# Attention scores with keys on partitions and no row maximum, with the old code behind a branch, in a kernel of four attention layers

## The chip, the cores and the metric

One core of a Trainium2 chip. The metric is the device time of one execution in microseconds (us). Each kernel ran several times; medians are given. The numbers of a profile come from one profiled execution. The granted clock is the share of TensorE's full clock in the profile's clock records; "half clock" is 0.50 there. One run of the kernel before took 6055 us at a clock of 0.63 and is left out as slow.

## The reference

The input x is 4 x 512 channels x 1024 positions, fp32. Four layers update it one after another:

```python
# layer 0: attention, 8 heads of 64
qkv = x^T @ Wp.T + bp;  attn = softmax(q k^T * 64**-0.5);  x = x + (attn v) @ Wo.T + bo
# layer 1: linear attention, softplus features of width 64, gated by max + mean of each channel
x = x + gamma * (Qf @ (Kf^T V)) / (Qf @ (sum(Kf) + 1e-6))
# layer 2: layer norm over channels, attention with 1 head of 512, projection, residual
# layer 3: group norm (32 groups), attention with 4 heads of 128, projection, residual
```

`softmax` is jax.nn.softmax, so it is right for scores of any size.

## The kernel before

x stays on chip with channels on partitions. Per batch, q and k are made with channels on partitions and v with tokens on partitions. The attention holds scores with **queries** on partitions, so that the row maximum and the row sum run along the free axis, and must then transpose the normalised weights for the product with v:

```python
        def scores(i):                      # one tile of 128 queries x 1024 keys
            ...
            ps = ps_sc.tile([P, S], F32, tag="sc", name="sc")
            for half in range(NTB):
                for n, c in enumerate(chunks):
                    nc.tensor.matmul(ps[:, bass.ts(half, TB)],                       # L186
                        lhsT=q[p0:p1, c, bass.ts(qb * QT + t, P)], rhs=k[p0:p1, c, bass.ts(half, TB)], ...)
            nc.vector.tensor_reduce(nmax, ps, AX.X, ALU.max, negate=True)            # L193
            nc.scalar.activation(pr, ps, AF.Exp, bias=nmax, accum_out=rs)            # L196
            nc.vector.reciprocal(ri, rs)
            nc.vector.tensor_scalar(pr, pr, ri, None, ALU.mult)                      # L199

        def transposes(i):
            for half in range(2):
                ps = ps_tr.tile([P, NT // 2, P], F32, tag="tr", name="tr")
                for j in range(NT // 2):
                    nc.tensor.transpose(ps[:, j, :], pr[:, ...], ident)              # L212
                ... copied to pt by ScalarE (L215) or VectorE (L217)

        def values(qb, h):                  # after four query tiles
            for c in chunks:
                ps = acc_tile()
                for j in range(NT):
                    nc.tensor.matmul(ps[p0:p1, :],                                   # L227
                        lhsT=v[:, j, c * P + p0 : c * P + p1], rhs=pt[...], ...)
                nc.scalar.activation(ots[qb][p0:p1, c, :], ps[p0:p1, :], AF.Identity, bias=...)

        def project_out(qb): ...            # 4 x 4 matmuls (L243) and x += (L248)
```

The projections are L141 (q, k) and L156 (v). The tiles that matmuls write are two accumulators of 512 columns (`acc`), two score tiles of 1024 and two transpose tiles of 512. `head_rows` gives layer 0's 64-wide heads partitions 0 to 63 or 64 to 127 of a chunk, so there the stationary operand of the scores is 64x128 and that of the values 128x64.

The framework orders the instructions of each engine at compile time, nearly as written, but not always.

Of the kernel before, what the change touches and what calls it, by code (L numbers as in the profile page):

```python
# [11 lines left out]

F32 = mybir.dt.float32
AF = mybir.ActivationFunctionType
ALU = mybir.AluOpType
AX = mybir.AxisListType

P = 128
B = 4
C = 512  # L20
S = 1024
NC = C // P  # channel chunks
NT = S // P  # token tiles
TB = 512  # token block
NTB = S // TB
QT = TB // P
M = 64  # feature width of the linear attention
GROUP = 16  # channels in a group of the group norm

# Vectors over channels, each stored as columns of 128.  # L30
COLS = [
    ("bqkv0", 12),
    ("bo0", 4),
# [8 lines left out]
COL = {}  # L42
for _name, _n in COLS:
    COL[_name] = sum(n for _, n in COLS[: len(COL)])
NCOLS = sum(n for _, n in COLS)


@with_exitstack
def conv_seq(ctx: ExitStack, tc: tile.TileContext, d: dict, out: bass.AP):
    """x stays on chip, channels on partitions, and the four layers update it in place."""  # L50
    nc = tc.nc

    const = ctx.enter_context(tc.tile_pool(name="const", bufs=1))
# [2 lines left out]
    work = ctx.enter_context(tc.tile_pool(name="work", bufs=1))  # L56
    small = ctx.enter_context(tc.tile_pool(name="small", bufs=4))
    PSUM = bass.MemoryType.PSUM
    ps_acc = ctx.enter_context(tc.tile_pool(name="ps_acc", bufs=2, space=PSUM))
    ps_sc = ctx.enter_context(tc.tile_pool(name="ps_sc", bufs=2, space=PSUM))  # L60
    ps_tr = ctx.enter_context(tc.tile_pool(name="ps_tr", bufs=2, space=PSUM))

    def acc_tile():
        return ps_acc.tile([P, TB], F32, tag="acc", name="acc")

# [1 line left out]
    def load_wqkv(src, split=False):  # L67
        t = wpool.tile([P, NC, 3 * C], F32, tag="wqkv", name="wqkv")
        v = src.rearrange("(c p) o -> p c o", p=P)
        if split:  # L70
            return t, v
        nc.sync.dma_start(t, v)
        return t

    def load_wo(src):
        t = wpool.tile([P, NC, C], F32, tag="wo", name="wo")
        nc.sync.dma_start(t, src.rearrange("(c p) o -> p c o", p=P))
        return t
# [22 lines left out]
    gamma = const.tile([P, 1], F32, name="gamma")  # L101
    nc.sync.dma_start(gamma, d["gamma"].partition_broadcast(P))

# [1 line left out]
    ident = const.tile([P, P], F32, name="ident")  # L105
    make_identity(nc, ident)
    ones = const.tile([P, P], F32, name="ones")
    nc.vector.memset(ones, 1.0)
    eps = const.tile([P, 1], F32, name="eps")
    nc.vector.memset(eps, 1e-5)  # L110
    # gmat[p, m] = 1/16 where p and m lie in the same group of 16 channels
    gmat = const.tile([P, P // GROUP, GROUP], F32, name="gmat")
    nc.vector.memset(gmat, 1.0 / GROUP)
    nc.gpsimd.affine_select(
# [8 lines left out]
    def col(name, c, p0=0, p1=P):  # L123
        return cols[p0:p1, COL[name] + c : COL[name] + c + 1]

# [1 line left out]
    def project_qkv(wqkv, bias, scale, src):  # L127
        """q (scaled) and k with channels on partitions, v with tokens on partitions.

        src(tb) gives the input as a [P, NC, TB] block. v's bias is added to the attention's  # L130
        output instead, as each row of the softmax sums to one.
        """
        q = work.tile([P, NC, S], F32, tag="q", name="q")
        k = work.tile([P, NC, S], F32, tag="k", name="k")
        v = work.tile([P, NT, C], F32, tag="v", name="v")
        for tb in range(NTB):
            xb = src(tb)
            for o in range(2 * NC):
                ps = acc_tile()
                for c in range(NC):  # L140
                    nc.tensor.matmul(  # L141
                        ps, lhsT=wqkv[:, c, bass.ts(o, P)], rhs=xb[:, c, :],
                        start=(c == 0), stop=(c == NC - 1),
                    )
                if o < NC:
                    nc.vector.tensor_scalar(  # L146
                        q[:, o, bass.ts(tb, TB)], ps, col(bias, o), scale, ALU.add, ALU.mult
                    )
                else:
                    nc.scalar.activation(  # L150
                        k[:, o - NC, bass.ts(tb, TB)], ps, AF.Identity, bias=col(bias, o)
                    )
            for t in range(QT):
                ps = acc_tile()
                for c in range(NC):
                    nc.tensor.matmul(  # L156
                        ps, lhsT=xb[:, c, bass.ts(t, P)], rhs=wqkv[:, c, 2 * C : 3 * C],
                        start=(c == 0), stop=(c == NC - 1),
                    )
                if t % 2:  # L160
                    nc.scalar.copy(v[:, tb * QT + t, :], ps)
                else:
                    nc.vector.tensor_copy(v[:, tb * QT + t, :], ps)  # L163
        return q, k, v

    def attention(b, q, k, v, heads, bias, wo, bo, hooks, last):
        hd = C // heads
        nk = max(1, hd // P)
        x = xs[b]
# [1 line left out]
        probs, pts, ots = {}, {}, {}  # L171

        def head_rows(h):
            """The chunks of channels that hold head h, and its partitions in them."""
            if hd >= P:
                return [h * nk + i for i in range(nk)], 0, P
            per = P // hd
            return [h // per], (h % per) * hd, (h % per + 1) * hd
# [70 lines left out]
                if last:  # L249
                    nc.sync.dma_start(xout[b, :, o, bass.ts(qb, TB)], xv)  # L250

        # The scores run two steps ahead of the transposes that need their softmax, and the
        # products with v one step behind the transposes.
        n, due = len(items), {}
        i = 0
        while i < n + 2 or due:
# [15 lines left out]
    def attention_layer(wqkv, wo, bias, bo, heads, norm=None, after_qkv=None, last=False):  # L272
        scale = float(C // heads) ** -0.5
        steps = NTB * heads * QT
        ready = {}

        def normed(b, tb):
            ready[b, tb] = norm(b, tb)

        if norm is not None:  # L280
            for tb in range(NTB):
                normed(0, tb)
        for b in range(B):
            if norm is None:
                src = lambda tb: xs[b][:, :, bass.ts(tb, TB)]
            else:
                src = lambda tb: ready.pop((b, tb))
            q, k, v = project_qkv(wqkv, bias, scale, src)
            hooks = {}
            if norm is not None and b + 1 < B:  # L290
                for tb in range(NTB):
                    hooks[steps // 2 + tb * steps // 4] = lambda tb=tb: normed(b + 1, tb)
            if b == B - 1 and after_qkv is not None:
                after_qkv()
            attention(b, q, k, v, heads, bias, wo, bo, hooks, last)

# [1 line left out]
    attention_layer(wqkv, wo, "bqkv0", "bo0", heads=8)  # L298

# [1 line left out]
    wqkv = load_wqkv(d["wqkv2"])  # L301
    wo = load_wo(d["wo2"])
    bv1 = work.tile([P, C], F32, tag="pr", bufs=2, name="bv1")
    nc.sync.dma_start(bv1, d["bv1"].partition_broadcast(P))

    def softplus(z, e, u, l):
        """z <- max(z, 0) + log1p(exp(-|z|)), with log1p(e) = ln(u) + (e - (u - 1)), u = 1 + e."""
        nc.vector.scalar_tensor_tensor(e, z, -1.0, z, ALU.mult, ALU.min)
        nc.scalar.activation(e, e, AF.Exp)
        nc.vector.tensor_scalar(u, e, 1.0, None, ALU.add)  # L310
        nc.scalar.activation(l, u, AF.Ln)
        nc.vector.scalar_tensor_tensor(u, u, 1.0, e, ALU.subtract, ALU.subtract)
        nc.vector.tensor_tensor(l, l, u, ALU.subtract)
        nc.vector.scalar_tensor_tensor(z, z, 0.0, l, ALU.max, ALU.add)

    def linear_attention(b):
        x = xs[b]
        # queries [M, S], channels on partitions
        qbuf = work.tile([P, NC, S], F32, tag="q", name="qbuf")
        qf = qbuf[:M, 0, :]  # L320
        for tb in range(NTB):
# [5 lines left out]
                )  # L327
            nc.scalar.activation(qf[:, bass.ts(tb, TB)], ps[:M, :], AF.Identity, bias=bq1)
        softplus(qf, qbuf[:M, 1, :], qbuf[:M, 2, :], qbuf[:M, 3, :])
        # keys [tokens, M]  # L330
        kbuf = work.tile([P, 4, NT, M], F32, tag="k", name="kbuf")
        kf = kbuf[:, 0]
        ps = acc_tile()
# [6 lines left out]
        for t in range(NT):  # L340
            nc.vector.tensor_tensor(kf[:, t, :], ps[:, bass.ts(t, M)], bk1, ALU.add)
        softplus(kf, kbuf[:, 1], kbuf[:, 2], kbuf[:, 3])
        # values [tokens, C], without their gate
        v = work.tile([P, NT, C], F32, tag="v", name="v1")
        for t in range(NT):
            ps = acc_tile()
# [3 lines left out]
                    start=(c == 0), stop=(c == NC - 1),  # L350
                )
            nc.vector.tensor_tensor(v[:, t, :], ps, bv1, ALU.add)
        # gate * gamma, a factor of each channel
        gate = small.tile([P, NC], F32, tag="gate", name="gate")
        gsum = small.tile([P, NC], F32, tag="gsum", name="gsum")
        nc.vector.tensor_reduce(gate, x, AX.X, ALU.max)  # L356
        nc.vector.tensor_reduce(gsum, x, AX.X, ALU.add)
        nc.vector.scalar_tensor_tensor(gate, gsum, 1.0 / S, gate, ALU.mult, ALU.add)
        nc.vector.tensor_scalar(gate, gate, gamma, None, ALU.mult)
        # keys x values, and the sums of the keys in all columns  # L360
        kv = work.tile([M, C], F32, tag="pt", bufs=3, name="kv")
        ps = acc_tile()
        for t in range(NT):
# [26 lines left out]
    for b in range(B):  # L390
        linear_attention(b)

# [1 line left out]
    def layer_norm(b, tb):  # L394
        x = xs[b][:, :, bass.ts(tb, TB)]
        xn = work.tile([P, NC, TB], F32, tag="xn", bufs=2, name="ln")
# [24 lines left out]
        after_qkv=lambda: wqkv3.append(load_wqkv(d["wqkv3"])),  # L421
    )

# [1 line left out]
    affine = {}  # L425

    def group_norm(b, tb):
        x = xs[b]
        if tb == 0:
            stats = small.tile([P, NC, NTB, nc.vector.BN_STATS_DIM], F32, tag="st", bufs=1, name="st")  # L430
            mv = small.tile([P, NC, 2], F32, tag="mv", bufs=1, name="mv")
            for c in range(NC):
                for t in range(NTB):
                    nc.vector.bn_stats(stats[:, c, t, :], x[:, c, bass.ts(t, TB)])
                nc.vector.bn_aggr(mv[:, c, :], stats[:, c, :, :].rearrange("p t s -> p (t s)"))
            # a group's variance: the mean of its channels' and the variance of their means
            g = gmat.rearrange("p a b -> p (a b)")
            ps = acc_tile()
            nc.tensor.matmul(
# [75 lines left out]
```

## Time and profile before

| | before |
|---|---|
| time, median | 4054.3 us |
| span of the profile | 4052.5 us |
| TensorE busy | 98% |
| VectorE, ScalarE busy | 38%, 24% |
| mean granted clock of TensorE | 0.976 |

The profile's groups read: line, engine, operation, tiles, shapes, count, then busy time, mean length of one, and idle time before them with what ended it. The mean length of a 512-column matmul in them is no pace: it is 0.59 to 0.65 us here, and inside a run the starts lie 0.429 us apart. The chain of what ended last reads: start, length, what, how many instructions. The stretches read: from and to, length, busy time of TensorE, its weight loads, VectorE, ScalarE and GpSimd with counts, then granted clock, and the share and rate of the transfers. The prediction below shows and reads these lines.

### The profile page before, as it was taken

The page shows a single profiled execution, that of the slowest core. Times are in us where ns is not written, and L with a number is a line of the kernel's source. Part 1 is how long each engine was busy: PE and PEld are TensorE (multiplying, and loading weights), DVE is VectorE, ACT ScalarE, POOL GpSimd, SP SyncE. Part 2 cuts the span into 40 slices and gives each one's busy share as a digit, 9 for nine tenths or more (in the row PEclk, how much of TensorE's full clock was granted, in tenths as well). Part 3 has the DMA queues.
Part 4 walks back from the last instruction along what each step waited for, and adds up shares of the span by engine and source line. Part 5 has one row for each costly group of instructions (what it writes and reads, how often), then busy time and mean ns, then how long its engine had stood idle before and what let it go on. Part 6 is the DMA issues. An engine that isn't in the chain of part 4 may idle for free.

```text
span 4052.5 us, 27875 instructions
## 1 busy us (share of the span) xinstructions
PE 3955.4 (98%) x11424; PEld 1781.6 (44%) x11424; DVE 1531.7 (38%) x2263; ACT 991.5 (24%) x1630; POOL 1.3 (0%) x8
## 2 busy tenths in 40 slices
PE   9999999999999999988889999999999999999999
PEld 3444444444444444434334444444444545445454
DVE  1555244533544255443332213121212624425244
ACT  1333133312332133311112112021111413214132
POOL 0000000000000000000000000000000000000000
PEclk9999989999999899988889999999999999999999
DMA  3000000000000000000000000000000000000000
GB/s 138 1 1 0 0 1 0 0 0 0 1 1 0 31 1 0 3 11 0 0 0 0 0 0 0 0 0 0 31 11 1 11 11 0 21 0 11 11 0 21
DMA packets 11823, 32.79 MB, mean 8 GB/s; under 512 B 1328, under 2 KB 1840, under 8 KB 11696
## 3 DMA queue, kind: packets, MB, share of 16 engines
q1 hardware_dynamic: 11696, 31.00, 2.0%
q8 instruction: 91, 1.49, 0.2%
q14 instruction: 36, 0.29, 0.0%
HBM read 22.61 MB, written 8.39 MB: 8 GB/s over the span
## 4 chain that ended last, share of the span: by engine, by line
PE 95%; DVE 3%; ACT 1%; DMA 0%; issue 0%; SPq 0%; ACTq 0%
PE sc L186 23%; PE acc L227 22%; PE acc L141 15%; PE tr L212 10%; PE acc L243 8%; PE acc L156 8%; PE acc L348 2%; PE acc L384 1%; PE acc L324 1%; PE acc L336 1%; PE acc L408 1%; PE acc L364 1%; DVE rd L380 1%; PE acc L399 1%; DVE pt L217 0%; DVE gate L356 0%
## 5 line engine op out<-in xcount | busy, mean ns | idle before, releaser
L186 PE MATMUL sc<-k,q 64*128 64x512 f32 (+1 forms) x2048 | 1010.0, 621 | 7.3 <-ACT pr L196 7.1
L227 PE MATMUL acc<-pt,v 128*64 128x512 f32 (+1 forms) x2048 | 910.1, 596 | 4.2 <-DVE pt L217 4.2
L193 DVE TENSOR_REDUCE nmax<-sc 128x1 f32<-128x1024 f32 x416 | 508.2, 1222 | 824.7 <-PE sc L186 822.1
L196 ACT ACTIVATE pr<-sc,nmax 128x1024 f32<-128x1024 f32 x416 | 464.2, 1116 | 357.9 <-PE tr L212 191.8
L227 PEld LDWEIGHTS acc<-pt,v 128*64 128x64 f32 (+1 forms) x2048 | 323.9, 164 | 507.4 <-issue 482.2
L212 PEld LDWEIGHTS tr<-ident,pr 128*128 128x128 f32 x3328 | 377.0, 144 | 365.1 <-issue 267.0
L186 PEld LDWEIGHTS sc<-k,q 64*128 64x128 f32 (+1 forms) x2048 | 357.0, 191 | 404.5 <-issue 378.7
L212 PE MATMUL tr<-ident,pr 128*128 128x128 f32 x3328 | 477.1, 283 | 18.1 <-DVE pr L199 10.4
L215 ACT COPY pt<-tr 128x512 f32<-128x512 f32 x416 | 242.4, 583 | 660.3 <-PE tr L212 557.1
L243 PE MATMUL acc<-ot,wo 128*128 128x512 f32 x768 | 335.7, 593 | 0.0
L199 DVE TENSOR_SCALAR pr<-pr,ri 128x1024 f32<-128x1024 f32 x416 | 310.8, 747 | 11.2 <-DVE ri L198 0.5
L217 DVE COPY pt<-tr 128x512 f32<-128x512 f32 x416 | 283.4, 681 | 20.8 <-PE tr L212 20.6
L150 ACT ACTIVATE k<-acc,cols 128x512 f32<-128x512 f32 x96 | 66.0, 687 | 734.8 <-PE acc L141 734.8
L233 ACT ACTIVATE ot<-acc,cols 64x512 f32<-64x512 f32 (+1 forms) x128 | 87.6, 684 | 645.5 <-PE acc L227 645.5
L163 DVE COPY v<-acc 128x512 f32<-128x512 f32 x48 | 33.2, 692 | 542.1 <-PE acc L156 542.1
L141 PE MATMUL acc<-x,wqkv 128*128 128x512 f32 x512 | 224.3, 597 | 11.1 <-DMA wqkv<-in_wqkv 9.2
L141 PE MATMUL acc<-gn,wqkv 128*128 128x512 f32 x512 | 223.0, 596 | 5.1 <-DVE gn L462 5.1
L243 PEld LDWEIGHTS acc<-ot,wo 128*128 128x128 f32 x768 | 144.0, 190 | 178.7 <-issue 178.2
L141 PE MATMUL acc<-ln,wqkv 128*128 128x512 f32 x512 | 221.0, 592 | 0.0
L248 DVE SCALAR_TENSOR_TENSOR x<-acc,cols,x 128x512 f32<-128x512 f32 x96 | 72.0, 750 | 394.0 <-PE acc L243 394.0
L146 DVE TENSOR_SCALAR q<-acc,cols 128x512 f32<-128x512 f32 x96 | 71.7, 749 | 278.8 <-PE acc L141 278.7
L141 PEld LDWEIGHTS acc<-x,wqkv 128*128 128x128 f32 x512 | 97.2, 191 | 136.2 <-issue 129.0
(93 smaller groups left out, 1709.9 us busy)
## 6 DMA issues: line engine op xcount, KB each, us to landing
out<-x SPq DMA_DIRECT2D x32, 256.0 KB, 2.0
x<-in_x SPq DMA_DIRECT2D x3, 2048.0 KB, 21.1
wqkv<-in_wqkv SPq DMA_DIRECT2D x2, 3072.0 KB, 10.6
wqkv<-in_wqkv SPq DMA_DIRECT2D x4, 768.0 KB, 8.5
wo<-in_wo SPq DMA_DIRECT2D x3, 1024.0 KB, 5.2
x<-in_x SPq DMA_DIRECT2D x4, 512.0 KB, 7.1
wv<-in_wv SPq DMA_DIRECT2D x1, 1024.0 KB, 17.5
wqk<-in_wqk SPq DMA_DIRECT2D x1, 256.0 KB, 19.7
```

What stands on the lines that cost most here:

```text
L141: nc.tensor.matmul(ps, lhsT=wqkv[:, c, bass.ts(o, P)], rhs=xb[:, c, :], start=(c == 0), stop=(c == NC - 1),)
L156: nc.tensor.matmul(ps, lhsT=xb[:, c, bass.ts(t, P)], rhs=wqkv[:, c, 2 * C : 3 * C], start=(c == 0), stop=(c == NC - 1),)
L186: nc.tensor.matmul(ps[:, bass.ts(half, TB)], lhsT=q[p0:p1, c, bass.ts(qb * QT + t, P)], rhs=k[p0:p1, c, bass.ts(half, TB)], start=(n == 0) ...
L193: nc.vector.tensor_reduce(nmax, ps, AX.X, ALU.max, negate=True)
L196: nc.scalar.activation(pr, ps, AF.Exp, bias=nmax, accum_out=rs)
L199: nc.vector.tensor_scalar(pr, pr, ri, None, ALU.mult)
L212: nc.tensor.transpose(ps[:, j, :], pr[:, bass.ts(half * (NT // 2) + j, P)], ident)
L215: nc.scalar.copy(dst, ps)
L217: nc.vector.tensor_copy(dst, ps)
L227: nc.tensor.matmul(ps[p0:p1, :], lhsT=v[:, j, c * P + p0 : c * P + p1], rhs=pt[j // (NT // 2)][:, j % (NT // 2), :], start=(j == 0), stop= ...
L233: nc.scalar.activation(ots[qb][p0:p1, c, :], ps[p0:p1, :], AF.Identity, bias=col(bias, 2 * NC + c, p0, p1),)
L243: nc.tensor.matmul(ps, lhsT=wo[:, c, bass.ts(o, P)], rhs=ot[:, c, :], start=(c == 0), stop=(c == NC - 1),)
```

## The change

The scores are turned: **keys** on partitions. Then exp's output is already what the product with v needs, and the transposes go. The sum over keys now lies across partitions: key tiles are added on VectorE and a matmul with ones adds over the partitions and writes the result to all of the head's rows. The row maximum is left out; if a sum's reciprocal leaves 1e-25 to 1e25 anywhere, a flag is set, and the whole old kernel (`general`) runs behind one branch. With these inputs the branch is not taken: that the guard catches what it should is not shown.

```diff
-    ps_acc = ctx.enter_context(tc.tile_pool(name="ps_acc", bufs=2, space=PSUM))
+    ps_acc = ctx.enter_context(tc.tile_pool(name="ps_acc", bufs=4, space=PSUM))
     ps_sc = ctx.enter_context(tc.tile_pool(name="ps_sc", bufs=2, space=PSUM))
-    ps_tr = ctx.enter_context(tc.tile_pool(name="ps_tr", bufs=2, space=PSUM))
 ...
+        def scores(i):
+            ps = ps_sc.tile([P, 2, TB], F32, tag="sc", name="sc")
+            for e in range(2):
+                for n, c in enumerate(chunks):
+                    nc.tensor.matmul(ps[:, e, :], lhsT=k[p0:p1, c, bass.ts(2 * jj + e, P)],
+                        rhs=q[p0:p1, c, bass.ts(qb, TB)], ...)
+            ex = work.tile([P, 2, TB], F32, tag="ex", bufs=6, name="ex")
+            nc.scalar.activation(ex, ps, AF.Exp, scale=scale)
+            ... sm = sum of the head's four ex (VectorE), then of its two halves
+        def total(qb, h):
+            ps = acc_tile()
+            nc.tensor.matmul(ps[p0:p1, :], lhsT=ones[:, p0:p1], rhs=sums.pop((qb, h))[:, 0, :],
+                start=True, stop=True)
+            nc.vector.reciprocal(rd[p0:p1, :], ps[p0:p1, :])
+        def look(rd, h):     # largest and smallest of rd into seen
+        def values(qb, h, jj):
+            for e in range(2):
+                nc.tensor.matmul(ps[p0:p1, :], lhsT=v[:, j, c * P + p0 : c * P + p1], rhs=ex[:, e, :], ...)
+            if jj == NJ - 1:
+                rd = total(qb, h)
+                nc.vector.tensor_tensor(ot[p0:p1, c, :], outs.pop((qb, h))[p0:p1, :], rd[p0:p1, :], ALU.mult)
+                look(rd, h)
 ...
+        # attention_layer, before the first projection: v's bias through wo, by matmul
+        for o in range(NC):
+            for c in range(NC):
+                nc.tensor.matmul(ps[:, 0:1], lhsT=wo[:, c, bass.ts(o, P)], rhs=col(bias, 2 * NC + c), ...)
+            nc.vector.tensor_tensor(bout[:, o : o + 1], ps[:, 0:1], col(bo, o), ALU.add)
 ...
-        conv_seq(tc, d, out)
+            fast(tc, d, out, bad)
+            taken = nc.values_load(bad[0:1, 0:1])
+            with tc.If(taken > 0):
+                general(tc, d, out)
```

The loop takes a step of two key tiles: the scores of step i, then the values of step i - 2. In layer 2 all values of a head come together (`all_values`). Cut are that function, the unchanged layers, and `general`, which is the kernel before.

## The prediction

> **What bounds the kernel now.** I read the page's busy shares first, then the chain that ended last, then the chain piece by piece, then the groups by form, then stretches by layer.
>
> The busy shares, the slices and the chain's shares by line:
>
> ```profile
> PE 3955.4 (98%) x11424; PEld 1781.6 (44%) x11424; DVE 1531.7 (38%) x2263; ACT 991.5 (24%) x1630; POOL 1.3 (0%) x8
> ...
> PE 95%; DVE 3%; ACT 1%; DMA 0%; issue 0%; SPq 0%; ACTq 0%
> PE sc L186 23%; PE acc L227 22%; PE acc L141 15%; PE tr L212 10%; PE acc L243 8%; PE acc L156 8%; PE acc L348 2%; PE acc L384 1%; PE acc L324 1%; PE acc L336 1%; PE acc L408 1%; PE acc L364 1%; DVE rd L380 1%; PE acc L399 1%; DVE pt L217 0%
> ```
>
> TensorE is the bound from end to end; VectorE and ScalarE have more than half of the span free. What leaves TensorE shortens the kernel, what leaves the others does not. Of what the change takes away only the transposes (tr, L212) are on the chain.
>
> The length of a matmul in the groups is a latency, not a pace, so I took paces from pieces of the chain (start, length, what):
>
> ```profile
> 53.02 27.47 PE acc L141 x64
> ...
> 202.27 1.91 PE sc L186 x4
> 204.18 1.02 PE tr L212 x8
> 205.20 1.91 PE sc L186 x4
> 207.11 1.02 PE tr L212 x8
> ...
> 214.00 7.01 PE acc L227 x16
> ...
> 2155.04 20.60 PE sc L186 x48
> ```
>
> The reader is to see three things. 27.47/64 = 0.429 us is the pace of a 512-column instruction, and 20.60/48 gives the same for layer 2's scores; each fp32 matmul of the program is two such instructions (x512 where the code has 256), 0.858 us. Second, the pace needs one shape after another: in layer 0, where the stationary operand is 64x128 for scores, 128x128 for transposes and 128x64 for values, four score instructions take 1.91 instead of 1.72 (0.19 lost on entering), sixteen values 7.01 instead of 6.87 (0.14 lost). Third, eight transposes take 1.02 us there; inside a run of them the starts lie 0.109 us apart (8 x 0.109 = 0.87, and 0.15 lost on entering).
>
> By form:
>
> ```profile
> L212 PE MATMUL tr<-ident,pr 128*128 128x128 f32 x3328 | 477.1, 283 | 18.1 <-DVE pr L199 10.4 <-ACT pt L215 5.4 <-DVE pt L217 2.3
> ...
> L411 DVE RECIPROCAL rstd<-rstd 128x512 f32<-128x512 f32 x8 | 26.8, 3353 | 30.7 <-ACT rstd L410 30.7
> ...
> L313 DVE TENSOR_TENSOR qbuf<-qbuf 64x1024 f32<-64x1024 f32 x4 | 4.8, 1208 | 0.0
> ```
>
> The first is what goes; the other two are the rates of what VectorE gets instead: 3.35 us for a reciprocal of 512 columns, 1.21 us for an fp32 addition of 1024.
>
> Stretches (length, busy of each engine, clock), one batch of layer 0's attention and the next, layer 1, then one batch each of layers 2 and 3:
>
> ```profile
> 94.30:448.00 353.70, 349.90 (x1113) 147.60 (x1113) 184.64 (x269) 120.39 (x209) 0.00 (x0) 0.99 0.00 1
> 520.30:882.00 361.70, 357.84 (x1113) 151.02 (x1114) 184.78 (x269) 120.43 (x209) 0.00 (x0) 0.96 0.00 1
> 1734.00:2072.00 338.00, 291.71 (x809) 126.79 (x808) 133.46 (x173) 47.39 (x53) 0.00 (x0) 0.83 0.01 2
> 2557.00:2799.00 242.00, 241.08 (x609) 109.40 (x608) 54.08 (x71) 38.78 (x58) 0.00 (x0) 1.00 0.00 0
> 3289.00:3543.00 254.00, 250.73 (x775) 124.06 (x774) 103.73 (x169) 71.64 (x119) 0.00 (x0) 1.00 0.02 9
> ```
>
> Layers 2 and 3 are packed. Layer 0 loses some clock soon after each attention starts, where TensorE waits for the first softmax, and layer 1 loses a lot around its reciprocals.
>
> [...]
>
> **The change part by part.** Scores keep their count and shape (keys and queries swap sides); values keep theirs.
>
> *Transposes go.* 416 score tiles x 8 = 3328: 2048 in layer 0, 256 in layer 2, 1024 in layer 3. At 0.109 that is 223 + 28 + 112 us.
>
> *Sums come.* One fp32 ones-matmul per (batch, half, head), 104 x 0.858 = 89 us: 55, 7 and 27 us by layer, all on the path.
>
> *Layer 0, per step.* Before, by the chain: 1.91 + 1.02 + 7.01/4 = 4.68 us on a clean stretch. After: scores 1.91, then four values 4 x 0.429 + 0.14 = 1.86, and a quarter of a sum 0.21: 3.98. Now values alternate with scores every step, so the 0.14 is paid four times as often as before. A batch is then 192 projections x 0.429 = 82.4, 64 x 3.98 = 255, output projection 64 x 0.429 = 27.5: 366 us with one for switches. Before, batches follow each other every 426 to 434 us (starts at 447.9, 881.9, 1308.0), 429 on the mean; that includes the waits for softmax and the half-clock spells, which I expect to vanish: exp needs only the score tile. Gain 63 a batch; I keep back 2 for new waits: 4 x 61 = **-245**.
>
> *Layer 3.* 253.3 a batch, all 128x128, no switches: -256 x 0.109 = -28, +16 x 0.429 = +7, about -1 of waits: 4 x 22 = **-88**.
>
> *Layer 2.* -64 x 0.109 = -7.0, +1.7: 4 x 5.3 = **-21**.
>
> *Layer 1.* Untouched but for four accumulators instead of two; the waits for its reciprocals stay: **-5**.
>
> *Output bias by matmul (bout).* 32 one-column instructions a layer, some 0.11 us each at full clock (the pace of the 64-column key matmuls, 7.36 us for 64), 0.2 at half: 3.5 to 7. They need wo. The first wo lands at 19 us, while projections started at 7; in the trace no projection of a next batch runs ahead of the output projection's accumulators, so I take it that accumulators are handed out in program order and that bout's four block the projections: +14 at the start. Layer 2's wo is long there: +4. Layer 3's can be loaded only after layer 2's last use and took 5.2 us; then bout, then the group norm's small matmuls that before began at once: +13. Together **+31**.
>
> *End.* The look at the extremes, a count, a register load and a branch over the general path, none of it beside other work: an estimate of **+10**.
>
> *VectorE and ScalarE.* Per head VectorE does 3 x 1.21 + 0.68 additions, 3.35 reciprocal, 0.69 product, 2 x 0.65 extremes: 9.7 us against TensorE's 4 x 3.98 = 15.9 in layer 0 and 14.6 in layer 3. Per step ScalarE's exp takes 1.1 of 3.4 to 4. Both stay off the path; max, scaling and copies that leave them are worth nothing by themselves.
>
> Sum: 4054 - 245 - 88 - 21 - 5 + 31 + 10 = 3736; I say **3730**.
>
> **The rivals.**
>
> *VectorE's chain becomes a wait.* The reciprocal of 3.35 us stands between a head's sum and its product. It would cost where nothing else is ready: at a batch's end, where sum, reciprocal and product take 4.8 us. For it: layer 1 waits on just this. Against: four accumulators let output projections start on the finished chunks. If it did cost, some 3 us at eight to twelve ends, 40 us with clock: 3770.
>
> *Shape changes double.* If the compile-time order interleaves scores and values one matmul at a time (the chain before has stretches of two scores and four transposes), the 0.33 us a step is paid twice: +85 us, 3815. Against: in the new code nothing makes a half step ready alone.
>
> *The half clock holds in layer 0.* Scores use 64 of 128 rows; before, the half clock came only with waits, and then lasted up to 27 us. Without waits I expect none, but if it held for half of layer 0, that is some 500 us and the gain is gone. I give it 2%.
>
> *Better than said.* The extra accumulators fill layer 1's gaps with the next batch and its clock stays up: up to 60 us less, 3670. Or bout hides: 20 less.
>
> **Range and chances.** Firm are counts times paces: -363 for transposes, +89 for sums. Uncertain are layer 0's waits, clock and order (some 80 of its 245), bout and end (41), layer 1. I take 3670 to 3800. Faster by 2% needs under 3973, 240 us of slack: 0.97; within 2%: 0.02; slower: 0.01.
>
> **What would show it.** Right: no transposes; PE still above 95% of the chain; batches of layer 0 every 366 us, of layer 3 every 231, of layer 2 every 237; in the chain, four scores of 1.91 alternating with values of 1.86; clock 1.00 in layer 0; layer 1 near 330; a first projection only after 20 us. Wrong: TensorE waiting for rd or the product (VectorE is late), score pieces of two, a clock under 0.97 in layer 0, layer 1 under 300, or more than 20 us after the last output.

One paragraph of the prediction is cut, because it told of more than the traces show; no term of the sum is cut (4054 - 245 - 88 - 21 - 5 + 31 + 10 = 3736). Three figures were estimates: 0.65 us for a look at the extremes (the profile after has 0.67), 0.2 us for a one-column instruction at half clock (0.21 to 0.22 in the profile after, under a clock record of 0.50: 30 in 6.54 us in layer 2, 32 in 6.86 us in layer 3), and the +10 for the end, with no run behind it (3.1 us, see "No guard").

## The result, and the profile after

The kernel after takes **3673.95 us** (3673.33 to 3675.21, four runs) against 4054.32 (4045.16 to 4061.96): ratio **0.9064**, 95% interval 0.9046 to 0.9081. A ratio here is the mean time of one kernel's fast runs over that of the other's fast runs of the same rounds, so it is not quite the ratio of the medians quoted. The output is correct.

The busy shares of the kernel after, and its chain by engine:

```profile
PE 3590.0 (98%) x8402; PEld 1456.5 (40%) x8402; DVE 1406.7 (38%) x1426; ACT 644.9 (18%) x718; POOL 0.9 (0%) x6
...
PE 97%; DVE 2%; DMA 1%; issue 0%; ACT 0%; SPq 0%; ACTq 0%
```

TensorE is the bound as before, with 3022 instructions fewer (3328 transposes gone; 208 for the sums, 96 for the output bias and 2 for the guard came). VectorE's busy share is unchanged at 38%: other work took the place of maximum, scaling and copies. Two of the new groups of the kernel after, the sums of layer 0 and their reciprocals:

```profile
L226 DVE RECIPROCAL rd<-acc 64x512 f32<-64x512 f32 x64 | 214.7, 3355 | 96.1 <-PE acc L221 96.1
...
L221 PE MATMUL acc<-sm,ones 128*64 128x512 f32 x128 | 66.8, 603 | 0.0
```

The stretches of both kernels, cut at the first projection, at layer 1's first matmul, at layer 2's first matmul and at layer 3's first projection; first before, then after:

```profile
7.00:1731.00 1724.00, 1707.06 (x5121) 724.88 (x5122) 758.53 (x1115) 510.74 (x880) 0.00 (x0) 0.98 0.03 10
1731.00:2048.50 317.50, 276.51 (x784) 120.83 (x784) 124.82 (x160) 40.50 (x43) 0.00 (x0) 0.84 0.01 4
2048.50:3034.20 985.70, 970.40 (x2438) 440.20 (x2437) 231.69 (x322) 153.94 (x232) 0.00 (x0) 0.99 0.01 5
3034.20:4052.50 1018.30, 1001.45 (x3084) 495.67 (x3084) 416.31 (x664) 285.00 (x474) 0.00 (x0) 1.00 0.02 9
```

```profile
26.30:1470.70 1444.40, 1438.76 (x3202) 495.44 (x3203) 680.34 (x588) 303.02 (x320) 0.00 (x0) 1.00 0.02 6
1470.70:1779.50 308.80, 273.92 (x785) 121.28 (x785) 125.03 (x160) 40.52 (x43) 0.00 (x0) 0.84 0.01 4
1779.50:2753.80 974.30, 959.75 (x2260) 429.87 (x2260) 228.30 (x274) 118.52 (x152) 0.00 (x0) 0.99 0.01 5
2753.80:3672.20 918.40, 910.72 (x2126) 403.02 (x2126) 372.07 (x398) 181.61 (x202) 0.00 (x0) 1.00 0.03 10
```

Differences: +19.3 until the first projection, -279.6 in layer 0, -8.7 in layer 1, -11.4 in layer 2 and the start of layer 3, -99.9 in layer 3: -380.3 in all. Layer 0's clock rose from 0.98 to 1.00; layer 1 keeps its waits (for qbuf 33.3 us before and 33.6 after, 8 each) and its 0.84.

The chain of the kernel after, in the middle of layer 0 (start, length, what):

```profile
203.56 1.91 PE sc L198 x4
205.47 1.86 PE acc L250 x4
207.33 1.91 PE sc L198 x4
209.24 0.57 PE acc L221
209.82 0.01 PE acc L250
209.82 0.42 PE acc L221
210.25 0.86 PE acc L250 x3
...
222.43 0.86 PE acc L221 x2
```

The steps are as predicted, 1.91 + 1.86. But the sum (L221) comes in two ways. At 222.43 it stands behind its own head's values and costs 0.86. At 209.24 it stands ahead of the next head's values and those come with it: sum and four values together end after 1.86 us, which is the time of the values alone. Starts lie 7 ns apart there. The profile gives 128*64 for both groups, rows times columns of the array that are in use; by the program, one head's instructions write rows 0 to 63 of their tile and the next one's 64 to 127. In each batch 7 of 16 sums stand so.

### The profile page after: what moved, and what is told of

It reads as the page before. It is cut to its first block, busy times and chain, and to the rows that moved or that the text cites. A ratio compares the mean times of both kernels' runs of the same rounds, so it can differ in the third digit from the quotient of the medians.

```text
span 3672.2 us, 19766 instructions
## 1 busy us (share of the span) xinstructions
PE 3590.0 (98%) x8402; PEld 1456.5 (40%) x8402; DVE 1406.7 (38%) x1426; ACT 644.9 (18%) x718; POOL 0.9 (0%) x6
## 4 chain that ended last, share of the span: by engine, by line
PE 97%; DVE 2%; DMA 1%; issue 0%; ACT 0%; SPq 0%; ACTq 0%
PE sc L198 25%; PE acc L250 18%; PE acc L154 18%; PE acc L169 9%; PE acc L283 9%; PE acc L271 6%; PE acc L401 3%; PE acc L221 3%; PE acc L437 2%; PE acc L377 1%; PE acc L389 1%; PE acc L417 1%; PE acc L461 1%; DVE rd L433 1%; PE acc L452 1%; PE acc L324 1%
## 5 line engine op out<-in xcount | busy, mean ns | idle before, releaser
L198 PE MATMUL sc<-q,k 64*128 64x512 f32 (+1 forms) x2048 | 968.4, 603 | 0.7 <-ACT ex L205 0.7
L250 PE MATMUL acc<-ex,v 128*64 128x512 f32 (+1 forms) x1536 | 731.8, 600 | 0.0
L205 ACT ACTIVATE ex<-sc 128x1024 f32<-128x1024 f32 x416 | 426.0, 1024 | 1405.7 <-PE sc L198 1341.1
L198 PEld LDWEIGHTS sc<-q,k 64*128 64x128 f32 (+1 forms) x2048 | 365.8, 188 | 572.0 <-issue 380.6
L209 DVE TENSOR_TENSOR sm<-ex 128x1024 f32<-128x1024 f32 x104 | 127.3, 1225 | 825.1 <-ACT ex L205 824.9
L226 DVE RECIPROCAL rd<-acc 64x512 f32<-64x512 f32 (+1 forms) x104 | 349.0, 3355 | 126.8 <-PE acc L221 126.6
L250 PEld LDWEIGHTS acc<-ex,v 128*64 128x64 f32 (+1 forms) x1536 | 217.0, 154 | 443.5 <-issue 441.4
L213 DVE TENSOR_TENSOR sm<-sm,ex 128x1024 f32<-128x1024 f32 x208 | 250.8, 1206 | 125.5 <-ACT ex L205 122.4
L271 PE MATMUL acc<-ex,v 128*128 128x512 f32 x512 | 221.0, 592 | 0.0
L169 PE MATMUL acc<-wqkv,x 128*128 128x512 f32 x256 | 111.2, 592 | 0.0
```

The source lines that it names most:

```text
L169: nc.tensor.matmul(ps, lhsT=xb[:, c, bass.ts(t, P)], rhs=wqkv[:, c, 2 * C : 3 * C], start=(c == 0), stop=(c == NC - 1),)
L198: nc.tensor.matmul(ps[:, e, :], lhsT=k[p0:p1, c, bass.ts(2 * jj + e, P)], rhs=q[p0:p1, c, bass.ts(qb, TB)], start=(n == 0), stop=(n == len ...
L205: nc.scalar.activation(ex, ps, AF.Exp, scale=scale)
L209: nc.vector.tensor_tensor(sm, exps[qb, h, 0], ex, ALU.add)
L213: nc.vector.tensor_tensor(sm, sm, ex, ALU.add)
L226: nc.vector.reciprocal(rd[p0:p1, :], ps[p0:p1, :])
```

## The experiments

Eleven kernels ran. "Distance of batches" is the time from one batch's first projection to the next one's, read from the starts in the trace; of three in a layer the second and third are given (before: the range of all).

| kernel | median us | ratio to before | layer 0 distance | layer 3 distance |
|---|---|---|---|---|
| before | 4054.3 | 1 | 426 to 434 | 253 to 255 |
| before, no maximum | 3975.6 | 0.981 | 413.1 | 250.9 |
| **after** | 3674.0 | 0.9064 | 360.6 | 227.2 |
| two accumulators | 3717.1 | 0.9175 | 362.4 | 232.7 |
| sums in 128 columns | 3709.2 | 0.9155 | 368.7 | 227.2 |
| late output bias | 3658.3 | 0.9033 | 360.6 | 227.2 |
| no guard | 3698.9 | 0.9126 | 367.1 | 227.2 |
| groups of two steps | 3602.8 | 0.8889 | 342.3 | 227.2 |
| pairs of heads | 3186.5 | 0.7861 | 238.5 | 227.2 |
| pairs, late bias | 3165.6 | 0.781 | 238.5 | 227.2 |
| pairs, bias spread | 3159.4 | 0.7795 | 238.5 | 227.2 |

The kernel after ran twice more as a base on the chips of the other runs (3675.28 and 3674.49 us):

> The changed kernel again, as the base for the runs beside it on the same chip. Both theories: 3674 us within 3, layer 0's batches 360.6 us apart.

> The changed kernel once more, as the base for the kernel without its guard on the same chip: 3675 us within 3.

### The row maximum alone

```diff
-            nmax = small.tile([P, 1], F32, tag="nmax", name="nmax")
-            nc.vector.tensor_reduce(nmax, ps, AX.X, ALU.max, negate=True)
-            nc.scalar.activation(pr, ps, AF.Exp, bias=nmax, accum_out=rs)
+            nc.scalar.activation(pr, ps, AF.Exp, accum_out=rs)
```

> The kernel before without the row maximum alone; transposes and all else stay. Theory (the maximum is beside the path on the mean, but it lengthens the chain score, maximum, exp, scaling, transpose, on which TensorE waits at each start and in layer 0's steps, and these waits bring the half clock): 20 to 60 us less, 3990-4035, with fewer or shorter half-clock spells in layer 0. Rival (VectorE is idle for more than half of the span, so its work is worth nothing): 4048-4060.

It took 3975.58 us (3975.27 to 3977.23): 79 less than before, more than the theory's 20 to 60; the interval of the ratio (0.978 to 0.984) straddles 2%. The rival is out. A stretch of layer 0's second batch, before (10 us shorter than the batch), then without the maximum (4 us longer than the batch); the clocks are what to compare, 0.97 and 1.00:

```profile
448.00:872.00 424.00, 420.78 (x1259) 178.91 (x1260) 182.10 (x277) 127.69 (x220) 0.00 (x0) 0.97 0.00 1
```

```profile
424.00:841.00 417.00, 414.59 (x1290) 181.41 (x1289) 129.94 (x218) 123.11 (x220) 0.00 (x0) 1.00 0.00 1
```

No half clock is left in layer 0 (before, the clock records hold two spells of 10.2 and two of 27.3 us at half, 37.5 us lost), and the batches come every 413.1 us, which is nearly the clean sum of the prediction's 4.68 us a step (64 x 4.68 + 82.4 + 27.5 = 409.4). VectorE had 508 us of maxima in a span of 4052, and yet they cost 79: the maximum lies in the chain score, maximum, exp, scaling, transpose, and TensorE waited for the end of that chain at each start and now and then in a step (before, 10.4 us in 8 waits of transposes for the scaled weights and 7.1 us in 8 of scores for exp; without the maximum 2.8 us and none in the list). These waits are the smaller part: idle time of TensorE falls by only 1.5 to 2.1 us a batch. The compile-time order changed too. Counted in the two traces, a batch had 187 changes of the stationary operand's shape, many of them around pieces of two scores and four transposes, and has 143 now; at some 0.165 us each, an estimate (the mean of the 0.19 and 0.14 that the prediction read from the chain), that is 7 us. With 9.4 us of half clock this makes up about the 17 us a batch that layer 0 gained. So the run shows what the maximum was worth in this order of instructions, not a cost of the wait alone.

### Two accumulators

```diff
-    ps_acc = ctx.enter_context(tc.tile_pool(name="ps_acc", bufs=4, space=PSUM))
+    ps_acc = ctx.enter_context(tc.tile_pool(name="ps_acc", bufs=2, space=PSUM))
```

> Two accumulators instead of four. Theory (the chain sum, reciprocal 3.35, product 0.69 us is hidden only because other accumulators are free): TensorE waits 1.2 to 2.9 us for nearly each of the 96 heads and halves of layers 0 and 3; 3790-3950, with idle time of the value matmuls put down to the product. Rival (score tiles two steps ahead hide the chain by themselves): 3674-3690.

It took 3717.06 us, 42 more than the kernel after: a third of the least that the theory allowed, and more than the rival allowed. The waits of TensorE with two accumulators (us in total, times, longest):

```profile
PE acc L283 <- DVE rd L226: 27.6, 8, 3.5
PE sc L198 <- ACT ex L205: 16.6, 17, 1.0
```

and with four:

```profile
PE acc L283 <- DVE ot L257: 5.6, 4, 1.4
```

The theory of a wait at each head is wrong: the compile-time order moved scores ahead, and they fill the time of the reciprocal. But that layer 0's distance grows by 1.8 us only is a sum of effects of both signs, because the order is another one. No sum runs beside values now (6.0 us a batch lost, see the next experiment), TensorE is idle for 8.7 us a batch instead of 1.4, and 1.7 us go to half clock. In return a batch has 92 changes of shape instead of 126, and where scores of two heads follow each other they overlap, seven in 1.93 us where 3.2 would be needed one after another (7 x 0.429 + 0.19):

```profile
209.41 1.93 PE sc L198 x7
```

So scores that use different halves of the array's rows (64*128 in the profile) overlapped already here. What does show cleanly is the end of a batch, where no scores are left: 3.5 us at the output projection of each of the eight batches of layers 0 and 3, against 1.4 us at four of them with four accumulators. A spell of half clock of 3.4 to 6.8 us comes with each of the eight. By stretch, between the profiles: 7 us in layer 0, 7 in layer 1, 8 from there to layer 2's first projection (not taken apart), 24 in layer 3.

### Sums in all 128 columns

```diff
-                ps[p0:p1, :], lhsT=ones[:, p0:p1], rhs=sums.pop((qb, h))[:, 0, :],
+                ps, lhsT=ones, rhs=sums.pop((qb, h))[:, 0, :],
```

> The ones-matmul of layer 0 writes all 128 columns instead of the head's 64. Theory (a head's sum, in one half of the array's columns, really runs at the same time as the next head's values in the other half, as two starts 7 ns apart in the trace say): the overlap is lost, 14 of 16 sums a batch x 0.43 us, and a change of shape is added; layer 0's batch goes from 360.6 to some 370 us, the kernel to 3704-3720. Rival (the two starts are an artefact of the records and each sum already costs its full 0.86 us): only the changes of shape are added, at most some 5 us a batch: 3680-3695.

It took 3709.15 us, 34 more than the kernel after on the same chip, and the distance is 368.7 us: the theory's side. (The text counted 14 sums with one hidden instruction of 0.43 us each; the trace has 7 sums with both hidden. The product, 6.0 us a batch, is the same.) Where the sum stands ahead of values it now takes 1.05 us by itself in the chain and the values 1.86 behind it, 2.91 instead of 1.86; nine others take 1.05 instead of 0.86. 7 x 1.05 + 9 x 0.19 = 9.1 us; measured 8.1.

### The late output bias

```diff
             q, k, v = project_qkv(wqkv, bias, src)
+            if b == 0:
+                make_bout()          # was ahead of the loop over batches
```

> The output bias is made after the first batch's projections instead of before them. Theory (its matmuls stand in front of the projections, wait for wo twice and run at half clock): the first projection starts near 7 us instead of 26, layer 3's gap falls from 19 to some 7 us, the bias runs at 0.11 instead of 0.22 us an instruction; 3640-3650. Rival (TensorE would have waited there for other loads and for the norm anyway): above 3665.

It took 3658.28 us, 17 less, between the two. The first projection starts at 6.9 us and layer 3's gap is 7 us, as the theory said. But the bias brings a cost of its own at the new place. The 32 one-column instructions with two scores between them and two behind, and the stretch that follows:

```profile
91.60:96.40 4.80, 4.80 (x36) 3.95 (x34) 0.48 (x3) 0.58 (x1) 0.00 (x0) 1.00 0.01 3
96.90:107.10 10.20, 10.20 (x13) 3.42 (x12) 2.43 (x2) 3.07 (x3) 0.00 (x0) 0.50 0.00 0
```

TensorE counts as busy in the first stretch, and still the clock is 0.50 for the next 10.2 us, inside the first attention, where it is busy too (10.20 of 10.20).

### No guard

```diff
-                look(rd, h)
 ...
-    (extremes, count, flag)
-            taken = nc.values_load(bad[0:1, 0:1])
-            with tc.If(taken > 0):
-                general(tc, d, out)
```

> The changed kernel without the guard: no look at the extremes, no count, no branch and no general path (right for these inputs, not for all). Theory (the looks lie beside TensorE's work, only the last count, register load and branch are seen): the time after the last output falls from 6.3 to 3 us, all else as it was; 3 to 5 us less, 3670-3672. Rival (VectorE's 140 us of looks delay the products that TensorE waits for): 15 us or more less.

It took 3698.93 us (3698.39 to 3699.62): **24 more**, which neither theory allowed. The end is as the theory said: 2.9 us from the last VectorE instruction to the end of the span, against 6.0 with the guard. The rest is in layer 0, 367.1 instead of 360.6 us a batch. Its chain at the place of a sum:

```profile
210.35 1.05 PE sc L198 x2
211.40 1.00 PE acc L221 x2
212.40 1.05 PE sc L198 x2
```

Without the looks the compile-time order put 7 of 16 sums between the scores of a step. There a sum overlaps with nothing and adds a pair of changes of shape: 7 x (0.86 + 0.33) = 8.3 us a batch; measured 6.5, and the wait of 1.4 us at a batch's end, which this trace no longer has, makes up most of the rest. No pair of starts under 12 ns is left in this trace's layer 0. So the guard's own cost is seen only as 3 us at the end; its looks happened to shape an order worth 24 us.

### Groups of two steps

Layer 0 only: scores of steps 2g and 2g + 1, then the values of the two steps before, and a head's sum right ahead of the next head's values (the code is shortened).

```diff
+            for i in two: scores(i)
+            for i in two:
+                if last_head and (i - 2 >= n or items[i - 2][2] == 0):
+                    finish(*last_head)       # sum, reciprocal, product of the head before
+                values(*items[i - 2])
```

> Layer 0 of the changed kernel takes two steps of scores, then two steps of values, and a head's sum one group later; the work is the same, changes of shape are half. Theory (each pair of changes costs 0.33 us[...]): 32 instead of 64 pairs a batch, 10.5 us a batch less, 350 us a batch, 3630-3636. Rival (the loss belongs to each small matmul or to waits for exp, not to the change of shape): 3665-3680.

It took 3602.78 us, 72 less than the kernel after, and 342.3 us a batch, 18.3 less. Its chain:

```profile
201.03 3.63 PE sc L198 x8
204.66 0.57 PE acc L221
...
211.87 3.58 PE acc L250 x8
```

Eight scores take 3.63 = 8 x 0.429 + 0.20 and eight values 3.58 = 8 x 0.429 + 0.15: one loss for each change of shape, not for each matmul. That gives 32 x 0.335 = 10.7 us, as expected. What the expectation lacked is that this order also puts 15 of 16 sums ahead of the other half's values; 8 more hidden sums x 0.86 = 6.9. Together 17.6 of the 18.3.

The starts of matmuls and weight loads in the profiles before and after show where the loss lies. Inside a run of 512-column instructions a weight load starts 0.43 us ahead of its matmul; the first one after a change starts only 2 ns ahead of it. That first matmul starts 0.09 us late, whatever the shape. The second starts another 0.10 us late where the operand has 128 columns (scores, output projections) and 0.05 us where it has 64 (values), but also 0.05 to 0.06 us at the transposes before, whose operand has 128. What causes either part, no run here shows.

### Pairs of heads

Layer 0 only. Heads 2m and 2m + 1 lie in the two halves of chunk m; their matmuls alternate, those of the two sums too, and reciprocal and product are made once for both.

```diff
+            for e in range(2):
+                for hh, (p0, p1) in enumerate(((0, 64), (64, 128))):
+                    nc.tensor.matmul(ps[:, hh, :], lhsT=k[p0:p1, m, bass.ts(2 * jj + e, P)],
+                        rhs=q[p0:p1, m, bass.ts(qb, TB)], start=True, stop=True)
 ...
+                    nc.tensor.matmul(ps[p0:p1, :], lhsT=v[:, j, m * P + p0 : m * P + p1],
+                        rhs=exs[e][:, hh, :], start=(j == 0), stop=(j == NT - 1))
```

> Layer 0 takes two heads at a time: score matmuls alternate between the two halves of the array's rows, value and sum matmuls between the two halves of its columns. Theory (matmuls in different halves run at the same time; each fp32 product is two instructions in the same half, so four products take five instruction times instead of eight): a step for two heads 1.19 times 3.86 = 4.6 us instead of 7.5, a batch some 265-275 us instead of 360.6, the kernel 3290-3330. Rival one (only column halves overlap, as the trace has shown so far): 3450-3500. Rival two (no overlap): half of the changes of shape go, 3630.

It took **3186.47 us** (3185.41 to 3187.04), 0.7861 of before, and 238.5 us a batch. Its chain:

```profile
156.92 1.92 PE sc L304 x8
158.84 1.87 PE acc L329 x8
160.71 0.86 PE acc L337 x4
```

Eight score instructions of two heads take 1.92 us where eight of one head took 3.63; eight values 1.87 instead of 3.58; two sums 0.86. Both rivals are out: halves of the rows overlap as well as halves of the columns. The theory was too careful: both instructions of an fp32 product overlap with both of the other half's (starts 6 to 7 ns apart in each pair), so a step is 3.79 us, not 4.6. Half of the 256 scores and half of the 256 values at 0.429 us are 110 us, half of the changes of shape are 10, and the wait at the batch's end is nearly gone: that is the 122 us a batch.

### Pairs with the late bias, and with the bias spread

> Pairs of heads and the late output bias together. Theory (the two act in different stretches): the two gains add up, e7 less 25 to 33 us: 3260-3305 if e7 is 3290-3330. Rival (with a faster layer 0 other waits, VectorE's among them, take up part): less than 15 us below e7.

3165.60 us: 21 less than pairs alone, between 25 to 33 and 15. In the waits of both kernels with pairs around it (pairs alone, bias spread) none of TensorE's in layer 0's attention is over 1.1 us in total, so VectorE takes nothing; part of the gain is lost again to half clock after the bias. The next kernel makes the bias in four chunks of eight instructions, one in each of the first attention steps (`if b == 0 and 1 <= i <= NC: make_bout(i - 1)`), with the former beside it on the same chip (3165.03 us):

> The kernel with pairs of heads and the late bias once more, as the base for the next one on the same chip: 3165.6 us within 3.

> As the one beside it, but the output bias's one-column matmuls are made a chunk of eight instructions at a time, among the first steps of the attention, not 32 in a row after the projections. Theory (a run of one-column matmuls[...] brings the half clock, which the trace shows at 97.5, 1387.7 and 2329.8 us for 3.4 us each): these spells vanish, 4 to 8 us less, 3157-3162. Rival (the half clock there comes from the change of stage, not from the bias): the same time within 2 us, spells stay.

3159.42 us (3158.72 to 3160.38), 5.6 less. The same 3.5 us in the former kernel (its first run), just after its bias, and in this one, with the first chunk of eight in them:

```profile
97.50:101.00 3.50, 3.50 (x9) 1.12 (x7) 0.09 (x1) 2.05 (x2) 0.00 (x0) 0.52 0.00 0
```

```profile
97.50:101.00 3.50, 3.50 (x20) 1.66 (x16) 1.69 (x3) 0.66 (x1) 0.00 (x0) 1.00 0.00 0
```

The clock stays at 1.00, here and at the two other places. This is the fastest kernel: 0.7795 of before (0.7774 to 0.7815), 515 us under the changed kernel, with the same guard and the same arithmetic but for the order in which the sums over keys are added.

## Why the prediction was right or wrong

The prediction was right: 3674 lies in 3670 to 3800, though at its edge. The gain was 380 us, and 324 had been forecast. That it still fell inside is partly luck: 24 us of the surplus come from an overlap that the prediction had ruled out ("all on the path"), and the two reasons that it gave for a time near 3670 (layer 1's clock staying up, the output bias hidden) did not come about: layer 1 kept 0.84, and the bias cost what was said.

- *TensorE is the bound, before and after*: right, 95% and 97% of the chain.
- *The step of layer 0, 1.91 and 1.86*: right to the hundredth, in the chain. That a change of shape costs it, and not each matmul, is shown by the groups of two steps; by what mechanism is not shown (see there).
- *Sums, "all on the path"*: this is the term that was mis-sized. In layer 0, 7 of 16 ran beside the next head's values: 4 x 7 x 0.86 = 24 us. The sums in 128 columns took it away (8.1 us a batch) and the pairs of heads showed how far it goes.
- *Layer 0, -245*: -279.6, so 35 more. 24 are the hidden sums, 8 the 2 a batch that was held back for waits, and 8 come from the base: the four batches before took 431 us on the mean (1724/4), not 429. Against them stand 1.4 us at each batch's end for which TensorE did wait.
- *"max, scaling and copies that leave them are worth nothing by themselves"*: wrong, and at odds with the prediction's own sum, which let the waits and the half clock of layer 0 go. The maximum alone was worth 79 us, 17 a batch in layer 0 and 2.4 a batch in layer 3, by the order of instructions and the clock as well as by waits.
- *Layer 3, -88*: 253.3 became 227.2, 26 a batch instead of 22. The counts gave 21 of it, the maximum 2.4. Of the remaining 2 to 3, 1.8 are idle time of TensorE that the transposes' chain had left: 3.3 us a batch before, 1.8 without the maximum, none after; the prediction had put about 1 for all waits.
- *Layer 2, -21, and layer 1, -5*: 242.2 became 235.4 a batch, so -27; layer 1 -8.7, of which 7 are the accumulators (with two, its stretch is 316.1 us again, before 317.5, after 308.8).
- *Output bias, +31*: the first projection came at 26.3 us and layer 3's gap grew from 7 to 18.9 us, as said. Moving it was worth 17 us, since it then costs half clock and some 0.11 us an instruction (24 in 2.73 us) elsewhere; the sum of 31 was not far off.
- *End, +10*: 3.1 us (6.0 against 2.9 without the guard). Count, register load and branch together are cheaper than the estimate.
- *The rivals*: VectorE's chain as a wait is real, at the batch's end only, 1.4 us with four accumulators and 3.5 with two. Changes of shape did not double; without the guard they rose from 126 to 140 a batch. No half clock in layer 0.

So of the 380 us, removing the maximum alone gives 79, and turning the scores with all that goes with it the other 302 (3975.6 to 3674.0). These are differences of whole kernels, not shares that would add up in any order.

## What to carry to other kernels

Read the pace of matmuls from the chain, and look for what breaks it: each change of the stationary operand's shape cost 0.14 to 0.20 us here, so group what has one shape. Where heads use half of the rows or of the columns, let matmuls of the two halves follow each other: with half of the shape changes gone as well it was worth 488 us here, more than the change that was studied. And work on an engine with time to spare can still be in the chain that the bound engine waits for, or shape the order of its instructions; take it away alone and measure.
